# Choosing experts for two token blocks at a time in an attention and mixture-of-experts kernel

## The chip, the core and the metric

The kernel runs on one core of a Trainium2 chip. The metric is the device time of one launch in microseconds (us). A core has five engines that run side by side, each through its own instruction stream in order: TensorE (PE, matrix products), VectorE (DVE), ScalarE (ACT), GpSimd (POOL), and SyncE (SP), which here issues DMAs. Engines wait for one another by semaphores.

## What is computed

The reference is one transformer layer in fp32 on 4096 tokens of width 256: attention over the whole causal sequence, and then a mixture of 8 experts of which each token takes 2.

```python
x = x + attention(layernorm(x), Qw, Kw, Vw)          # one head, causal
h = layernorm(x) @ W_in + b_in
probs = softmax(h @ W_gate + b_gate)                 # 8 experts
topv, topi = top_k(probs, 2)
topv = topv / topv.sum(-1, keepdims=True)            # the two shares
mid = relu(einsum('nd,edh->neh', h, W1) + b1)        # expert width 1024
eout = einsum('neh,ehd->ned', mid, W2) + b2
moe = sum over the two chosen experts of share * eout
out = x + moe @ W_out + b_out
```

## The kernel before

**Tiles and stages.** The 4096 tokens are 8 blocks of 512 (`NB`), each of 4 tiles of 128 tokens (`TPB`). Queries go in 16 groups of 256, two to a block; group `g` belongs to block `b = g // 2`, and `q = g % 2`. The main loop (L1036) runs over the groups. In each round it issues the scores of the next group (`scores`, L500, products `ps` at L516), a transposition of the running maxima and the subtraction of the maximum (`finish`, L554: `pt`, the reduction `m` at L563, `pmax`, the subtractions L572 and L578, Exp on ACT), and then the weighted sums of the present group (`attend`, L585, products `po` at L593, with rescaling at L605 and L607).

**What goes with the first group of a block** (`q == 0`). `enter(b - 1)` (L314) takes the normalized rows of the block before, forms `h` and the 8 logits of each token in one product (`ph`, L323) and adds the biases on DVE: the logits to `lg` (L333), the rows to `hr`, which SP writes to DRAM. Behind `attend` come the projection and the values of the next block (`pq` L472, `pv` L487), and then `route(b - 1)` (L347), then the statistics of block `b + 2`.

**`route`** chooses the experts of one block. Its DVE instructions work on all four tiles at once, as 128 partitions by 4 tokens by 8 experts, thus 32 columns:
- L360 to L375: the largest logit, its subtraction, an Exp on ACT (L362), twice the largest probability with a one-hot row of the expert that has it (`hot`; ties go by `rank`), and `both`, the sum of the two. Fourteen of these instructions follow one from another.
- L377 to L381: `past`, the running count of tokens per expert and partition; it begins with `seen` of the block before, and each further tile needs the one before it. The last one is the next `seen`.
- L384 and L389: two products on PE into `pk`, which turn `both` and `past` into each token's place in the list of its expert.
- L393 to L402: the place is added to the expert's first slot (`first`), picked out by `hot`, summed, and cast to integers `ati`.
- L404: eight scatters per block by POOL, which write the number of the assignment to its slot in DRAM.
- L416 to L419: the shares of the two experts.

The small tiles of `route` have two buffers. Block 6 is routed inside the last block's sums (`find`, L1072) and block 7 in the expert stage (L1209).

**Order.** The sequence of the text is what the compiler's scheduler starts from; it moves instructions within an engine by dependencies and by its own estimate of when each is ready. Some are held in program order by hand (`keep_in_program_order`). An engine then executes its order strictly.

**After the loop's start for block 7.** `early = seen` (L1051) takes the counts of blocks 0 to 5; `plan("a", ...)` (L1052) builds from them a table of work pieces of 256 slots. The expert stage (L1177) then runs over the pieces: fetch slots, gather rows, two products with the expert's weights (`pm`, `pe`), scatter. Last come the output products (`pa`, `pf`).

Of the kernel before, what the change touches and what calls it, by code (L numbers as in the profile page):

```python
# [10 lines left out]
F32 = mybir.dt.float32  # L11
I32 = mybir.dt.int32
AF = mybir.ActivationFunctionType
ALU = mybir.AluOpType
# [3 lines left out]
P = 128  # L18
# [6 lines left out]
SH = 128  # L25
SQR = 64
TOPK = 2
LINE = 16
SQ = 32
LATE = 2  # L30
# [7 lines left out]
def preln_attention_moe_kernel(  # L38
# [18 lines left out]
    nc = tc.nc  # L57

    _, S, D = x.shape
    NE, _, FF = W1.shape  # L60
    NT = S // P
    NB = S // TB
    TPB = TB // P
# [24 lines left out]
    const = ctx.enter_context(tc.tile_pool(name="const", bufs=1))  # L88
    stream = ctx.enter_context(tc.tile_pool(name="stream", bufs=1))
    dram = ctx.enter_context(tc.tile_pool(name="dram", bufs=1, space=bass.MemoryType.DRAM))  # L90
    attn = ctx.enter_context(tc.tile_pool(name="attn", bufs=1))
# [218 lines left out]
    share = [const.tile([P, NT], F32, tag=f"share{k}", name=f"share{k}") for k in range(TOPK)]  # L310
    seen = const.tile([P, NE], F32, tag="seen0", name="seen0")
    nc.gpsimd.memset(seen, 0.0)

    def enter(b, zT, pool, behind=False):  # L314


        hr = pool.tile([P, TPB, D], F32, tag="hr", name=f"hr{b}", bufs=1)

        lg = pool.tile([P, TPB, NE], F32, tag="lg", name=f"lg{b}", bufs=2)
        for j in range(TPB):  # L320
            ph = ps_mm(f"ph{b}_{j}")
            for c in range(ND):
                done = nc.tensor.matmul(  # L323
                    ph[:, :DG],
                    lhsT=zT[:, c, ts(j, P)],
                    rhs=win_sb[:, c, :],
                    start=(c == 0),
                    stop=(c == ND - 1),
                )
                if behind:  # L330
                    tc.keep_in_program_order(done)
                    behind = False
            nc.vector.tensor_tensor(lg[:, j, :], ph[:, D:DG], bgate_bc, ALU.add)  # L333
            nc.vector.tensor_tensor(hr[:, j, :], ph[:, :D], bin_bc, ALU.add)
        for k in range(TOPK):
            put = nc.sync.dma_start(
                out=rows[ts(b, TOPK * TB), :].rearrange("(t p k) d -> p t k d", p=P, k=TOPK)[
                    :, :, k, :
                ],
                in_=hr,  # L340
            )
            if b == NB - 1:
                tc.add_to_no_dep_group("last", put.ins)

        return lg

    def route(b, lg, seen, pool, behind=False):  # L347


        def small(name, w=1):  # L350
            return pool.tile([P, TPB, w], F32, tag=name, name=f"{name}{b}", bufs=2)

        def wide(a):
            return a.to_broadcast([P, TPB, NE])


        top = [small(f"top{k}") for k in range(TOPK)]
        hot = [small(f"hot{k}", NE) for k in range(TOPK)]
        prob, best = small("prob", NE), small("best")
        nc.vector.tensor_reduce(best, lg, AX.X, ALU.max)  # L360
        nc.vector.tensor_tensor(lg, lg, wide(best), ALU.subtract)
        nc.scalar.activation(prob, lg, AF.Exp)  # L362
        left = prob
        for k in range(TOPK):
            nc.vector.tensor_reduce(top[k], left, AX.X, ALU.max)
            nc.vector.tensor_tensor(hot[k], left, wide(top[k]), ALU.is_equal)
            nc.vector.tensor_tensor(hot[k], hot[k], rank, ALU.mult)
            nc.vector.tensor_reduce(best, hot[k], AX.X, ALU.max)
            nc.vector.tensor_tensor(hot[k], hot[k], wide(best), ALU.is_equal)
            if k == 0:  # L370
                left = small("left", NE)
                nc.vector.scalar_tensor_tensor(left, hot[0], -2.0, prob, ALU.mult, ALU.add)

        both = small("both", NE)
        nc.vector.tensor_tensor(both, hot[0], hot[1], ALU.add)  # L375
        past = small("past", NE)
        nc.vector.tensor_copy(past[:, 0, :], seen)  # L377
        for j in range(1, TPB):
            nc.vector.tensor_tensor(past[:, j, :], past[:, j - 1, :], both[:, j - 1, :], ALU.add)
        now = const.tile([P, NE], F32, tag=f"seen{b + 1}", name=f"seen{b + 1}")  # L380
        nc.vector.tensor_tensor(now, past[:, TPB - 1, :], both[:, TPB - 1, :], ALU.add)  # L381
        pk = ps_tr(f"pk{b}") if behind else ps_o(f"pk{b}")
        pkv = pk[:, : TPB * NE]
        done = nc.tensor.matmul(  # L384
            pkv, lhsT=before, rhs=both.rearrange("p t e -> p (t e)"), start=True, stop=False
        )
        if behind:
            tc.keep_in_program_order(done)
        nc.tensor.matmul(  # L389
            pkv, lhsT=ones, rhs=past.rearrange("p t e -> p (t e)"), start=False, stop=True  # L390
        )
        place = small("place", NE)
        nc.vector.tensor_tensor(  # L393
            place, pkv.rearrange("p (t e) -> p t e", e=NE), first, ALU.add
        )
        for k in range(TOPK):
            nc.vector.tensor_tensor(hot[k], hot[k], place, ALU.mult)
            at, ati = small(f"at{k}"), pool.tile(
                [P, TPB], I32, tag=f"ati{k}", name=f"ati{k}_{b}", bufs=2
            )  # L400
            nc.vector.tensor_reduce(at, hot[k], AX.X, ALU.add)
            nc.vector.tensor_copy(ati, at[:, :, 0])  # L402
            for j in range(TPB):
                put = nc.gpsimd.indirect_dma_start(  # L404
                    out=slots,
                    out_offset=bass.IndirectOffsetOnAxis(ap=ati[:, j : j + 1], axis=0),
                    in_=assign[:, TOPK * (b * TPB + j) + k :][:, :LINE],
                    in_offset=None,
                )

                tc.declare_no_dep(put.ins, group="slots", reason="slots are distinct")
                tc.add_to_no_dep_group("slots", put.ins)
                if b == NB - 1:
                    tc.add_to_no_dep_group("last", put.ins)
        tot = small("tot")
        nc.vector.tensor_tensor(tot, top[0], top[1], ALU.add)  # L416
        nc.vector.reciprocal(tot, tot)
        for k in range(TOPK):
            nc.vector.tensor_tensor(  # L419
                share[k][:, ts(b, TPB)], top[k][:, :, 0], tot[:, :, 0], ALU.mult  # L420
            )
        return now

# [564 lines left out]
    before = const.tile([P, P], F32, tag="before", name="before")  # L988
    make_upper_triangular(nc, before, 1.0, diag=False)

    rank = const.tile([P, TPB, NE], F32, tag="rank", name="rank")

    first = const.tile([P, TPB, NE], F32, tag="first", name="first")
    number = const.tile([P, NE], F32, tag="number", name="number")
    for e in range(NE):
        nc.gpsimd.memset(rank[:, :, e : e + 1], float(NE - e))
# [38 lines left out]
    fill, lg, got, hTs = [], None, {}, {}  # L1035
    for g in range(NT // KU):  # L1036
# [12 lines left out]
        if q == 0 and b == NB - 1:  # L1049
# [3 lines left out]
            for n in range(AHEAD + 1):  # L1053
                got[n] = fetch_rows(work[n])
        if q == 0 and b > 0:

            def send(behind=False):
                nonlocal lg
                lg = enter(b - 1, z1T, attn, behind)

            if b - 1 < TURNED[1]:
                turn(1, b - 1, rows1, z1T)
                send()
            else:
                between[5] = [partial(send, True)]
        if q == 0 and b == NB - 1:

            def fetch_first():
                for n in range(AHEAD):
                    got[n] += fetch_weights(work[n])  # L1070

            def find():  # L1072
                nonlocal seen
                seen = route(b - 1, lg, seen, attn, True)

            between[6], between[11] = [fetch_first], [find]
            weighed = AHEAD
        elif q == 0 and b + 1 < TURNED[0]:
            turn(0, b + 1, ahead, zT[b + 1])
        attend(g, row, between)  # L1080
        row = nxt
        if q == 0 and b + 1 < NB:
            project(b + 1)
            values(b + 1)
            if b > 0:
                seen = route(b - 1, lg, seen, attn)
        if q == 0 and b + 2 < NB:
            stats0(b + 2)
            by_dve = b + 2 >= TURNED[0]
# [87 lines left out]
    for n, item in enumerate(work):  # L1177
# [26 lines left out]
            following, behind = hidden(work[n + 1], got[n + 1], hTs.pop(n + 1), behind)  # L1204
        if n == 0:
            turn(1, NB - 1, rows1, z1T)
            lg = enter(NB - 1, z1T, attn)
        if n == 1:
            seen = route(NB - 1, lg, seen, attn)  # L1209
            tables["z"], seen = plan_late(seen, early)  # L1210
            tables["b"] = plan("b", seen, NBLK - NFULL, SB, SQR - 1, tables["a"][2])

            def twice(k):
                taken = const.tile([P, NE], F32, tag="twice" + k, name="twice" + k)
                nc.vector.tensor_scalar_mul(taken, tables[k][2], 2.0)
                return taken

            tables["c"] = plan("c", seen, NHALF, SH, SQR - 1, twice("b"))
            tables["d"] = plan("d", seen, 2 * NPAIR, SQR, SQR - 1, twice("c"))
# [59 lines left out]
```

## Time and profile before

| what | value |
|---|---|
| median of 3 runs | 1087.06 us (1086.69 to 1088.53) |
| profiled execution | 1081.01 us |
| its span, first to last instruction | 1079.2 us |
| mean granted TensorE clock | 1.000 |
| PE waits for `ph`, one at 53 us | 1.2 us |
| count products L384 and L389 | 16 and 16 records of 128x32, 2.6 and 3.0 us |
| scatters L404 | 64, 62.9 us on POOL, 983 ns each |
| one DVE instruction of 128x32 in `route` | 0.18 to 0.19 us |

The span is what lies between the first and the last instruction of one profiled execution; its own time has 1.8 us around it. A product in fp32 is two records in the trace. The duration of a matmul record covers its pipeline, so records overlap, and the distance from start to start is what a record costs the stream. Where an engine was idle before an instruction, the timeline gives the idle time and the event that ended it in brackets.

### The profile page before, as it was taken

To read this page: it belongs to the slowest core of one execution; us is meant where nothing else is said; L and a number is where in the kernel's file an instruction comes from. 1 tells how busy PE (TensorE), PEld (TensorE's weight loads), DVE (VectorE), ACT (ScalarE), POOL (GpSimd) and SP (SyncE) were. 2 spreads that over 40 slices of the span, in tenths; PEclk is the share of its full clock that TensorE was granted. 3 is DMA by queue.
4 is the path that set the end of the run, shared out by engine and by line. 5 is a ranking of instruction groups with operands and counts; after the bars stand their busy time and mean duration, and the time that the engine had idled before them with its cause. 6 is when DMAs were issued, how large, how long until landed. Compare 5 with 4: busy or idle time off the path is not lost. (4 is left out here: it accounts for less than half of the span.)

```text
span 1079.2 us, 15699 instructions
## 1 busy us (share of the span) xinstructions
PE 1069.7 (99%) x5013; PEld 889.7 (82%) x5013; DVE 728.9 (68%) x2260; ACT 332.2 (31%) x731; POOL 238.4 (22%) x293
## 2 busy tenths in 40 slices
PE   9999999999999999999999999999999999999998
PEld 6878888888888888888888887787878777777887
DVE  5777788778676658255774743858588876767636
ACT  2222333332332323242402222232322432323254
POOL 2122312103103010201132522232222332313110
PEclk9999999999999999999999999999999999999999
DMA  9111001001001001000645474888879796979285
GB/s 329 59 42 40 3 1 42 1 11 32 1 1 42 1 1 40 3 1 0 187 144 181 155 241 148 274 276 259 290 253 330 254 337 208 332 224 327 80 294 189
DMA packets 121416, 151.96 MB, mean 141 GB/s; under 512 B 25581, under 2 KB 101298, under 8 KB 121332
## 3 DMA queue, kind: packets, MB, share of 16 engines
q1 hardware_dynamic: 112404, 132.84, 37.6%
q0 software_dynamic: 8384, 17.58, 5.1%
q8 instruction: 40, 0.66, 0.2%
q10 hardware_dynamic: 544, 0.52, 0.1%
q14 instruction: 44, 0.36, 0.1%
HBM read 124.79 MB, written 26.38 MB: 140 GB/s over the span
## 5 line engine op out<-in xcount | busy, mean ns | idle before, releaser
L593 PE MATMUL po<-v,s 128*128 128x257 f32 x1056 | 237.8, 380 | 0.0
L516 PE MATMUL ps<-qT,zT 128*128 128x256 f32 x1088 | 233.6, 374 | 0.0
L516 PEld LDWEIGHTS ps<-qT,zT 128*128 128x128 f32 x1088 | 203.4, 191 | 27.6 <-issue 1.3
L593 PEld LDWEIGHTS po<-v,s 128*128 128x128 f32 x1056 | 197.4, 190 | 26.2
L525 ACT COPY s<-ps 128x512 f32<-128x512 f32 x120 | 70.2, 585 | 170.7 <-PE ps L516 131.2
L948 PE MATMUL pe_a<-w_a,mid_a 128*128 128x256 f32 x544 | 121.6, 381 | 0.0
L881 PE MATMUL pm_a<-hT_a,w_a 128*128 128x256 f32 x544 | 120.0, 380 | 0.0
L948 PEld LDWEIGHTS pe_a<-w_a,mid_a 128*128 128x128 f32 x544 | 102.9, 190 | 18.7 <-issue 5.6
L890 ACT ACTIVATE mid_a<-pm_a,c_a 128x256 f32<-128x256 f32 x136 | 64.2, 472 | 169.3 <-PE pm_a L881 147.6
L881 PEld LDWEIGHTS pm_a<-hT_a,w_a 128*128 128x128 f32 x544 | 103.6, 190 | 13.8
L575 ACT ACTIVATE s<-s 128x512 f32<-128x512 f32 x120 | 71.7, 629 | 83.4 <-DVE s L572 83.1
L531 DVE TENSOR_TENSOR mx<-ps,mx 128x512 f32<-128x512 f32 x91 | 62.9, 691 | 50.8 <-ACT s L525 48.0
L861 DVE STREAM_TRANSPOSE hT_a<-h_a 32x128 f32<-32x128 f32 x272 | 82.2, 302 | 4.0
L404 POOL DMA_INDIRECT slots<-assign,ati x64 | 62.9, 983 | 84.2 <-DVE ati L402 65.6
L572 DVE TENSOR_TENSOR s<-s,pmax 128x512 f32<-128x512 f32 x120 | 73.1, 682 | 7.3 <-PE pmax L568 7.3
L957 POOL DMA_INDIRECT parts<-y_a,slot_a x34 | 34.2, 1006 | 168.2 <-DVE y_a L956 139.0
L853 DVE STREAM_TRANSPOSE mid_c<-raw_c 32x256 f32<-32x256 f32 x128 | 55.8, 436 | 1.9
L948 PE MATMUL pe_b<-w_b,mid_b 128*128 128x256 f32 x256 | 56.8, 380 | 0.0
L881 PE MATMUL pm_b<-hT_b,w_b 128*128 128x256 f32 x256 | 56.6, 380 | 0.0
L948 PEld LDWEIGHTS pe_b<-w_b,mid_b 128*128 128x128 f32 x256 | 48.6, 190 | 9.3 <-issue 2.6
L881 PEld LDWEIGHTS pm_b<-hT_b,w_b 128*128 128x128 f32 x256 | 48.7, 190 | 6.5
L890 ACT ACTIVATE mid_b<-pm_b,c_b 128x256 f32<-128x256 f32 x64 | 30.1, 471 | 63.0 <-PE pm_b L881 63.0
(283 smaller groups left out, 1232.9 us busy)
## 6 DMA issues: line engine op xcount, KB each, us to landing
w_a<-in_L_ffn_W_dram SPq DMA_DIRECT2D x68, 512.0 KB, 5.0
w_d<-in_L_ffn_W_dram SPq DMA_DIRECT2D x48, 512.0 KB, 5.4
w_c<-in_L_ffn_W_dram SPq DMA_DIRECT2D x32, 512.0 KB, 6.9
w_b<-in_L_ffn_W_dram SPq DMA_DIRECT2D x32, 512.0 KB, 7.4
rows<-hr SPq DMA_DIRECT2D x16, 512.0 KB, 4.1
yp<-parts SPq DMA_DIRECT2D x14, 512.0 KB, 11.2
x<-in_L_attn_x_dram SPq DMA_DIRECT2D x7, 512.0 KB, 7.0
out_dram<-ot SPq DMA_DIRECT2D x14, 256.0 KB, 5.2
```

The source lines that it names most:

```text
L404: put = nc.gpsimd.indirect_dma_start(out=slots, out_offset=bass.IndirectOffsetOnAxis(ap=ati[:, j : j + 1], axis=0), in_=assign[:, TOPK * ( ...
L516: nc.tensor.matmul(ps[:, u * QB + lo : (u + 1) * QB], lhsT=zT[kt // TPB][:, d, ts(kt % TPB, P)], rhs=qT[b][:, d, q * QB + lo : (q + 1) * Q ...
L525: nc.scalar.copy(flat, ps)
L531: done = nc.vector.tensor_tensor(mx, ps, old, ALU.max)
L572: nc.vector.tensor_tensor(s, s, pm[:, :QB].unsqueeze(1).to_broadcast([P, KU, QB]), ALU.subtract)
L575: nc.scalar.activation(s, s, AF.Exp)
L593: nc.tensor.matmul(po[u][:, : D + 1], lhsT=ss[c][:, k, ts(u, P)], rhs=vb[kt // TPB][:, kt % TPB, :], start=(kt == 0), stop=(kt == g * KU + u),
L853: pin(do())
L861: pin(do())
L881: nc.tensor.matmul(pm[:, :SB], lhsT=w1[c][:, ts(f, P)], rhs=hT[:, c, :], start=(c == 0), stop=(c == ND - 1),)
L890: nc.scalar.activation(mid[f // 2][:, f % 2, :], pm[:, :SB], AF.Relu, bias=c1[:, f : f + 1])
L948: nc.tensor.matmul(pe[ts(j, rest), :D], lhsT=mid[f][:, ts(u, P)][:, ts(j, rest)], rhs=w2[f // (NF // 2)][:, f % (NF // 2), :], start=(f == 0),
```

## The change

Blocks 0 and 1, 2 and 3, and 4 and 5 are routed together, at the place where blocks 1, 3 and 5 were routed. Blocks 6 and 7 are routed alone as before. A new constant `ROUTED = 2` gives the number of blocks in a set.
- The logits of two blocks lie in one tile `lg` of 8 tokens by 8 experts per partition, and `enter` is given its half.
- `route(b, n, ...)` takes `n` blocks: its instructions have 64 columns where `n` is 2, the chain of `past` has 7 additions where it had 3 for each block, `pk` is one pair of products of 64 columns, and 16 scatters follow one another.
- The small tiles have room for two blocks and one buffer where they had two.
- `rank` and `first`, which POOL fills at the start, are twice as wide.

```diff
+ROUTED = 2
...
-    def enter(b, zT, pool, behind=False):
+    def enter(b, zT, pool, lg, behind=False):
...
-        lg = pool.tile([P, TPB, NE], F32, tag="lg", name=f"lg{b}", bufs=2)
...
+    def logits(b):
+        return attn.tile([P, ROUTED * TPB, NE], F32, tag="lg", name=f"lg{b}", bufs=2)
+
+    def route(b, n, lg, seen, pool, behind=False):
+
+        nt = n * TPB
 
         def small(name, w=1):
-            return pool.tile([P, TPB, w], F32, tag=name, name=f"{name}{b}", bufs=2)
+            t = pool.tile([P, ROUTED * TPB, w], F32, tag=name, name=f"{name}{b}", bufs=1)
+            return t[:, :nt, :]
...
-        for j in range(1, TPB):
+        for j in range(1, nt):
             nc.vector.tensor_tensor(past[:, j, :], past[:, j - 1, :], both[:, j - 1, :], ALU.add)
-        now = const.tile([P, NE], F32, tag=f"seen{b + 1}", name=f"seen{b + 1}")
-        nc.vector.tensor_tensor(now, past[:, TPB - 1, :], both[:, TPB - 1, :], ALU.add)
+        now = const.tile([P, NE], F32, tag=f"seen{b + n}", name=f"seen{b + n}")
+        nc.vector.tensor_tensor(now, past[:, nt - 1, :], both[:, nt - 1, :], ALU.add)
         pk = ps_tr(f"pk{b}") if behind else ps_o(f"pk{b}")
-        pkv = pk[:, : TPB * NE]
+        pkv = pk[:, : nt * NE]
...
-            nc.vector.tensor_copy(ati, at[:, :, 0])
-            for j in range(TPB):
+            nc.vector.tensor_copy(ati[:, :nt], at[:, :, 0])
+            for j in range(nt):
                 put = nc.gpsimd.indirect_dma_start(
...
-                share[k][:, ts(b, TPB)], top[k][:, :, 0], tot[:, :, 0], ALU.mult
+                share[k][:, b * TPB :][:, :nt], top[k][:, :, 0], tot[:, :, 0], ALU.mult
...
-    rank = const.tile([P, TPB, NE], F32, tag="rank", name="rank")
-
-    first = const.tile([P, TPB, NE], F32, tag="first", name="first")
+    rank = const.tile([P, ROUTED * TPB, NE], F32, tag="rank", name="rank")
+
+    first = const.tile([P, ROUTED * TPB, NE], F32, tag="first", name="first")
...
+            if (b - 1) % ROUTED == 0:
+                lg = logits(b - 1)
 
             def send(behind=False):
-                nonlocal lg
-                lg = enter(b - 1, z1T, attn, behind)
+                enter(b - 1, z1T, attn, lg[:, (b - 1) % ROUTED * TPB :][:, :TPB, :], behind)
...
-                seen = route(b - 1, lg, seen, attn, True)
+                seen = route(b - 1, 1, lg[:, :TPB, :], seen, attn, True)
...
-            if b > 0:
-                seen = route(b - 1, lg, seen, attn)
+            if b > 0 and b % ROUTED == 0:
+                seen = route(b - ROUTED, ROUTED, lg, seen, attn)
...
-            lg = enter(NB - 1, z1T, attn)
+            lg = logits(NB - 1)
+            enter(NB - 1, z1T, attn, lg[:, :TPB, :])
...
-            seen = route(NB - 1, lg, seen, attn)
+            seen = route(NB - 1, 1, lg[:, :TPB, :], seen, attn)
```

More of the change, by code (lines that the diff above doesn't have):

```diff
@@ L343, in enter @@
                 tc.add_to_no_dep_group("last", put.ins)
-        return lg
-    def route(b, lg, seen, pool, behind=False):
+    def logits(b):
+        return attn.tile([P, ROUTED * TPB, NE], F32, tag="lg", name=f"lg{b}", bufs=2)
+    def route(b, n, lg, seen, pool, behind=False):
+        nt = n * TPB
         def small(name, w=1):
-            return pool.tile([P, TPB, w], F32, tag=name, name=f"{name}{b}", bufs=2)
+            t = pool.tile([P, ROUTED * TPB, w], F32, tag=name, name=f"{name}{b}", bufs=1)
+            return t[:, :nt, :]
         def wide(a):
-            return a.to_broadcast([P, TPB, NE])
+            return a.to_broadcast([P, nt, NE])
         top = [small(f"top{k}") for k in range(TOPK)]
@@ L366, in route @@
             nc.vector.tensor_tensor(hot[k], left, wide(top[k]), ALU.is_equal)
-            nc.vector.tensor_tensor(hot[k], hot[k], rank, ALU.mult)
+            nc.vector.tensor_tensor(hot[k], hot[k], rank[:, :nt, :], ALU.mult)
             nc.vector.tensor_reduce(best, hot[k], AX.X, ALU.max)
@@ L393, in route @@
         nc.vector.tensor_tensor(
-            place, pkv.rearrange("p (t e) -> p t e", e=NE), first, ALU.add
+            place, pkv.rearrange("p (t e) -> p t e", e=NE), first[:, :nt, :], ALU.add
         )
@@ L398, in route @@
             at, ati = small(f"at{k}"), pool.tile(
-                [P, TPB], I32, tag=f"ati{k}", name=f"ati{k}_{b}", bufs=2
+                [P, ROUTED * TPB], I32, tag=f"ati{k}", name=f"ati{k}_{b}", bufs=1
             )
             nc.vector.tensor_reduce(at, hot[k], AX.X, ALU.add)
-            nc.vector.tensor_copy(ati, at[:, :, 0])
-            for j in range(TPB):
+            nc.vector.tensor_copy(ati[:, :nt], at[:, :, 0])
+            for j in range(nt):
                 put = nc.gpsimd.indirect_dma_start(
@@ L412, in route @@
                 tc.add_to_no_dep_group("slots", put.ins)
-                if b == NB - 1:
+                if b + n == NB:
                     tc.add_to_no_dep_group("last", put.ins)
```

## The prediction

> **What bounds the kernel now.** I read the page first, then the groups by shape, then TensorE's waits, then the timelines of TensorE (PE), VectorE (DVE) and GpSimd (POOL) around each set of choices.
>
> ```profile
> PE 1069.7 (99%) x5013; PEld 889.7 (82%) x5013; DVE 728.9 (68%) x2260; ACT 332.2 (31%) x731; POOL 238.4 (22%) x293
> ```
>
> PE is the bound over the whole span, and its order is fixed. What the change takes out of PE's stream, or makes PE wait for, is time; DVE's 32% of idle time hides what happens on DVE unless PE waits for it. The list of PE's waits is short, and two of its entries belong to the count products:
>
> ```profile
> PE pk L384 <- DVE both L375: 1.1, 1, 1.1
> PE pk L389 <- DVE past L379: 0.3, 1, 0.3
> ```
>
> Asked by windows, the first lies at 545 to 552 us (block 6, chosen alone before and after), the second at 60 to 80 us (block 0). In the timelines the columns are start, length, engine, line. Lengths of matmuls overlap (a 128x256 record is 0.38 long, yet one starts every 0.216 us), so I price by starts. Four places on PE:
>
> ```profile
> 70.75 0.30 PE L384 MATMUL pk<-both,before 128*128 128x32 f32 x2
> 71.32 0.41 PE L389 MATMUL pk<-past,ones 128*128 128x32 f32 x2 [0.27 <-DVE past L379]
> 71.56 2.62 PE L516 MATMUL ps<-qT,zT 128*128 128x256 f32 x11
> ...
> 118.11 0.30 PE L384 MATMUL pk<-both,before 128*128 128x32 f32 x2
> 118.25 0.39 PE L389 MATMUL pk<-past,ones 128*128 128x32 f32 x2
> 118.47 1.76 PE L516 MATMUL ps<-qT,zT 128*128 128x256 f32 x7
> ...
> 176.65 1.46 PE L516 MATMUL ps<-qT,zT 128*128 128x256 f32 x6
> 178.23 0.38 PE L384 MATMUL pk<-both,before 128*128 128x32 f32 x2
> 178.44 0.68 PE L516 MATMUL ps<-qT,zT 128*128 128x256 f32 x2
> 178.96 0.30 PE L389 MATMUL pk<-past,ones 128*128 128x32 f32 x2
> ```
>
> At 118 us nothing is waited for: from the first pk to the first ps is 0.36 us, and that ps takes 0.083 us over its usual 0.216 because its weights were not loaded ahead. At 70 us there is a wait inside. At 177 us the sixth ps starts at 177.73 (five steps of 0.216), so pk could start at 177.95 and starts at 178.23: 0.28 of wait.
>
> The DVE chain that feeds them, where it stands before work that PE wants (block 1), and where it has little slack (block 3):
>
> ```profile
> 107.20 0.19 DVE L375 TENSOR_TENSOR both<-hot,hot 128x32 f32<-128x32 f32 x1
> 107.43 0.57 DVE L379 TENSOR_TENSOR past<-past,both 128x8 f32<-128x8 f32 x3
> 108.03 0.17 DVE L381 TENSOR_TENSOR seen<-past,both 128x8 f32<-128x8 f32 x1
> 108.23 0.17 DVE L377 COPY past<-seen 128x8 f32<-128x8 f32 x1
> 108.31 0.42 DVE L563 TENSOR_REDUCE m<-pt 128x2 f32<-128x256 f32 x1
> ...
> 248.33 0.19 DVE L375 TENSOR_TENSOR both<-hot,hot 128x32 f32<-128x32 f32 x1
> 248.56 0.57 DVE L379 TENSOR_TENSOR past<-past,both 128x8 f32<-128x8 f32 x3
> ```
>
> Dependent small instructions start 0.20 to 0.22 us apart, independent ones about 0.09. At block 1, PE stands still some 0.30 us before its pmax transposes at 108.78 (four po from 107.61 are issued by 108.48), since m comes late behind the chain.
>
> [...] here four records of 128x32 take 0.446 us with the late ps, 0.111 each, so the loads set the price and not the 32 columns. [...] a pk that waits holds everything behind it, as at 70 us. [...] The trace has 182 to 188 for 128x32 rows and 211 to 220 for its 128x64 rows (L649, L655 of the plans): I take 0.03 us more for a doubled width.
>
> **The change part by part.** DVE and PE orders of both kernels agree except for the chains and the pk; SP's order is the same.
>
> *Removed on PE*: the products at blocks 0, 2 and 4, by the starts of single records in the trace. Block 0: from the first pk at 70.746 to the second ps record at 71.860 is 1.114, less one step of 0.216: 0.90 (0.43 of it wait). Block 2: from the ps record at 177.730 to the fourth ps record behind it at 179.399 (both pk lie between) is 1.67, less four steps, 0.86: 0.81 (0.28 of it wait). Block 4 is like 118 us: 0.45. Sum 2.15 us.
>
> *Kept but wider*: three pairs of 64 columns. 64 columns stream in less than the 0.109 us at which 128-column transposes start, which is below the weight load's 0.111. I take 0; the upper end is 27 ns more for each of six products, 0.16.
>
> *Pair of blocks 0 and 1* (at 104 us). Fourteen instructions from L360 to L375 get 64 wide: 14 x 0.03 = 0.42 later. But the new DVE order puts m behind the second past, where the old had three past, seen and the copy ahead: past 2 starts at 107.63, so m could follow at 107.72, 0.59 earlier. Net 0.17 earlier, and the 0.30 of PE wait shrinks by that. The other five past stand in front of the L572 subtractions: about 1 us, of which 0.53 was idle anyway (DVE waits for pmax there), so DVE runs some 0.3 behind PE's pace; the output rescaling L607 that frees PSUM for the pv products has about 0.45 of room (first one done 114.2, pv at 114.66). I take 0; lower cover would cost up to 0.15.
>
> *Pair 2, 3* (at 242 us). The chain is mixed with statistics and copies; both comes 0.42 later (end 248.94) and PE asks for it at 249.40: no wait. past is seven long instead of three, 4 x 0.20 = 0.80 more: it ended at 249.13 and ends at 250.35. The new PE order places one ps product between the two pk, so L389 is wanted 0.73 after L384, as at 178 us: 250.13. Wait 0.22. The split costs two switches instead of one, 0.08 (0.81 - 0.28 - 0.45). Together 0.30. Queued behind the waiting pk are only ps products; DVE's place L393 and what follows come about 1 us later, while the first PSUM tile that PE needs back from DVE (by L531) is four ps tiles, some 7 us, further on.
>
> *Pair 4, 5* (at 423 us). past would have ended near 428 against pk at 435.7: no wait.
>
> *DVE*: three chains less, about 28 instructions each; on no path but the waits named. *ACT*: three Exp less, three wider: none of them on PE's path. *POOL*: 64 scatters as before, but 16 in a row instead of 8. They start 1.265 us apart, so 20.2 us from 119.8 to 140.1. Behind them in the queue:
>
> ```profile
> 144.84 0.23 POOL L249 TENSOR_SCALAR ln1rstd<-ln1mv 128x4 f32<-128x4 f32 x1 [15.10 <-DVE ln1mv L243]
> ```
>
> It has 4.7 us of room; after the other pairs 16 and 30. *Startup memsets* of double width: POOL is idle for 7.35 us before 19.09. *Single buffers* in place of two: the last readers, the scatters, are done at least 30 us before the next writer (562 against 594 us for the two blocks chosen alone; over 80 us for the pairs). The last pair's scatters land near 458; the tables that read the slots are made from 508 on: nothing.
>
> *Sum*: -2.15 - 0.17 + 0.30 = -2.0 us. Against the profiled execution: 1081.01 (span 1079.2 and 1.8 around it) to 1079.0. The median of the runs shown is 6 us above that execution; I carry the difference over unscaled: 1087.06 - 2.0 = 1085.0.
>
> **The rivals.**
>
> A, as above, 1085.0, its own range 1084.4 to 1085.8 from the unknown ends (+0.16, +0.15, the wait at 250 us between 0 and 0.6): chance 0.58. It lies beside the bound of 0.2% (2.17 us), which is about what a measurement of this kernel can tell from no change; I give 0.30 beyond it and 0.28 within.
>
> B, more: with DVE freed, a larger wait that DVE causes shrinks as well, the 1.29 us at 545.7 before block 6's pk. For it: a DVE chain is what is late there. Against: that stretch has the same order and the same instructions, and DVE is driven by PE's own scores. 1083.7; chance 0.22, since the freed DVE touches many short waits that I can't list.
>
> C, less: the two removed waits (0.43 and 0.28) were cover for something, and PE stops at its next consumer instead. Then only three bare pairs of products go: -3 x 0.45 - 0.17 + 0.30 = -1.2, 1085.9. Against: at both places DVE loses work before that consumer. 0.10.
>
> D, slower: the doubled width costs DVE more than 0.03, at the two places where PE hangs on the chain. With w per instruction the sum is -2.15 + (14w - 0.59) + (14w + 0.80 - 1.00) + 0.08; it turns at w = 0.10. At double price, w = 0.185, it is +2.3: 1089.4. Against it are the 128x64 rows at 0.21 to 0.22. 0.10.
>
> That the change doesn't do what it says is ruled out by the order: six pk instructions fewer, 81 fewer on DVE.
>
> **How the numbers follow.** Faster 0.30 + 0.22 = 0.52; same 0.28 + 0.10 = 0.38; slower 0.10. The range, 1083.4 to 1086.9, holds A, B and C with the half us by which medians differ, and leaves out D and about as much at the tails.
>
> **What would show it.** Right: the wait at 70 us and the stop at 177.7 are gone, no pk stands at blocks 0, 2, 4; the pair of 64 columns without a wait takes 0.36 us to the first ps; a wait of 0.2 to 0.3 us for past near 248 us; 128x64 chain rows at 0.21 to 0.22. Wrong: chain rows above 0.3 us, a wait of over 1 us at the second pair or at pmax near 106 us, ln1rstd waiting for scatters, or a changed wait at block 6.

## The result, and the profile after

| | kernel before | changed kernel | ratio (95% interval) |
|---|---|---|---|
| comparison of the result, 6 runs each | 1088.61 us (1086.69 to 1092.04) | 1108.22 us (1106.2 to 1110.23) | 1.0181 (1.0166 to 1.0195) |
| profiled execution | 1081.01 us, span 1079.2 | 1106.74 us, span 1105.0 | |

The changed kernel is 1.8% slower, where 2 us less were forecast. One thing in the table bears on all that follows: the profile of the kernel before is of an execution of 1081 us, while its timed runs need 1087 to 1092 us. The experiments show that both belong to the same program under two conditions, which I call undisturbed (before at 1081.1) and disturbed (before at 1088.6). Each comparison below lay wholly within one of them, on one chip: undisturbed on the chips numbered 2, 14, 13 and 9, disturbed on those numbered 2 and 5.

The busy times of the page after, PE to POOL:

```profile
span 1105.0 us, 15591 instructions
PE 1077.1 (97%) x5001; PEld 889.7 (81%) x5001; DVE 720.5 (65%) x2182; ACT 331.3 (30%) x728; POOL 238.0 (22%) x293
```

The instructions went nearly as foreseen: 12 records fewer on PE, 3 fewer on ACT, and 78 fewer on DVE where 81 were forecast. Yet PE stands idle for 28 us where it had 9.5. The places that the prediction priced, in PE's timeline of the changed kernel (start, length, engine, line, operation, count):

```profile
69.19 1.46 PE L489 MATMUL pv<-vw,zT 128*128 128x256 f32 x6
70.49 2.32 PE L518 MATMUL ps<-qT,zT 128*128 128x256 f32 x10
...
116.85 0.33 PE L386 MATMUL pk<-both,before 128*128 128x64 f32 x2
117.02 0.39 PE L391 MATMUL pk<-past,ones 128*128 128x64 f32 x2
117.24 1.08 PE L518 MATMUL ps<-qT,zT 128*128 128x256 f32 x4
...
254.03 0.33 PE L386 MATMUL pk<-both,before 128*128 128x64 f32 x2
254.19 0.65 PE L518 MATMUL ps<-qT,zT 128*128 128x256 f32 x2
254.85 0.43 PE L391 MATMUL pk<-past,ones 128*128 128x64 f32 x2
```

The wait and the two products at 70 us are gone; from the first product of 64 columns to the first ps are 0.39 us. But the last stretch, for which PE asked at 249.40 in the kernel before, begins at 254.03, 4.6 us late instead of 2 early. The list of PE's waits in the changed kernel (us in total, times, longest) has entries that the kernel before doesn't have:

```profile
PE ps L518 <- DVE mx L533: 8.2, 3, 5.1
PE po L595 <- issue: 4.2, 6, 1.5
PE pm_a L883 <- ACT mid_a L892: 2.7, 1, 2.7
PE pt L560 <- issue: 2.2, 2, 1.1
```

"issue" means that nothing which the profile shows was waited for. How such a stop comes about is seen on ACT, which copies scores from PSUM behind PE. ACT's timeline of the changed kernel in the second row of 16 scatters, with the idle time before each copy and what ended it:

```profile
261.85 0.59 ACT L527 COPY s<-ps 128x512 f32<-128x512 f32 x1 [1.14 <-PE ps L518]
263.58 0.59 ACT L527 COPY s<-ps 128x512 f32<-128x512 f32 x1 [1.14 <-issue]
266.90 0.59 ACT L527 COPY s<-ps 128x512 f32<-128x512 f32 x1 [2.73 <-remote]
272.59 0.59 ACT L527 COPY s<-ps 128x512 f32<-128x512 f32 x1 [5.10 <-PE ps L518]
279.66 1.56 ACT L527 COPY s<-ps 128x512 f32<-128x512 f32 x3 [6.49 <-remote]
```

and PE's own timeline there:

```profile
264.24 7.93 PE L518 MATMUL ps<-qT,zT 128*128 128x256 f32 x36
273.95 1.57 PE L518 MATMUL ps<-qT,zT 128*128 128x256 f32 x8 [1.77 <-DVE mx L533]
275.36 0.60 PE L595 MATMUL po<-v,s 128*128 128x257 f32 x2
277.50 0.38 PE L595 MATMUL po<-v,s 128*128 128x257 f32 x1 [1.54 <-issue]
```

PE made scores up to 272 us, yet ACT's copies of them come 5.7 and 7.1 us apart where they came every 1.73 us. PE then runs out of free PSUM tiles (DVE's `mx` is late as well), and at last two of its own products start 1.9 us apart with nothing open. By 281 us ACT has caught up. POOL's timeline shows what else ended just before:

```profile
274.72 0.96 POOL L406 DMA_INDIRECT slots<-assign,ati  x1 [0.30 <-issue]
275.98 0.96 POOL L406 DMA_INDIRECT slots<-assign,ati  x1 [0.30 <-issue]
```

The sixteenth scatter starts at 275.98. Late copies and stops of PE stand at the other two rows of 16 as well. The scatters themselves keep their pace, 1.265 us from one to the next.

### The profile page after: what moved, and what is told of

Same layout as the page of the kernel before. It is cut to its first block, busy times and chain, and to the rows that moved or that the text cites. A ratio compares the mean times of both kernels' runs of the same rounds, so it can differ in the third digit from the quotient of the medians.

```text
span 1105.0 us, 15591 instructions
## 1 busy us (share of the span) xinstructions
PE 1077.1 (97%) x5001; PEld 889.7 (81%) x5001; DVE 720.5 (65%) x2182; ACT 331.3 (30%) x728; POOL 238.0 (22%) x293
## 5 line engine op out<-in xcount | busy, mean ns | idle before, releaser
L595 PE MATMUL po<-v,s 128*128 128x257 f32 x1056 | 242.0, 383 | 4.2 <-issue 4.2
```

The source lines that it names most:

```text
L595: nc.tensor.matmul(po[u][:, : D + 1], lhsT=ss[c][:, k, ts(u, P)], rhs=vb[kt // TPB][:, kt % TPB, :], start=(kt == 0), stop=(kt == g * KU + u),
```

## The experiments

Theories: BURST (a row of more than some eight scatters delays what other engines do), CHAIN (the 64-wide chain with its single buffers and later `past`), and others as they came up. Where two kernels are compared by PE's starts, the record starts of PE in the two traces are matched one by one, and the growth of their distance over a stretch is given.

### A pause between the scatters, first attempt

```diff
+                if n == ROUTED and k * nt + j in PAUSES:
+                    for _ in range(PAUSE):
+                        nc.gpsimd.tensor_tensor(idle, idle, half[:, :TPB], ALU.pow)
                 put = nc.gpsimd.indirect_dma_start(
```

`PAUSES` is (8,), (4, 8, 12) and (12,); `PAUSE` is 6, 2 and 6.

> The changed kernel, with a pause of six tiny powers on GpSimd (six by 1.04 us = 6.2 us by the row of ln0rstd) between scatter 8 and scatter 9 of each pair; nothing else. BURST (more than some 8 scatters without a pause delay the signals between the engines, and each scatter beyond costs time): the pause brings the three losses at 135-144, 271-281 and 462-475 us down to near nothing, 1086 to 1090 us. CHAIN (the 64-wide chain, its single buffers or its two products cost the time): all of that is unchanged, 1107 to 1109 us. HELD QUEUE (GpSimd occupied for longer delays what comes behind it): worse than the changed kernel, as the scatters end 6.2 us later, above 1109.

> The changed kernel with the same 6.2 us of pause for each pair, but as three pauses of two powers (2.1 us) after scatters 4, 8 and 12. If it is the mean rate of scatters over some 20 us that counts, as in the run with one pause, 1086 to 1090 us. If a backlog builds up from the first scatter on and needs several us of rest to drain, short pauses help less than the one long pause: between that run and 1108 us. CHAIN: 1107 to 1109 us.

> The changed kernel with the one pause of 6.2 us after scatter 12. BURST with a threshold near 8: scatters 9 to 12 still cost, a third to a half of the loss stays, 1093 to 1099 us. If it begins at 13 (the first stall in the changed kernel is seen 17 us after the first scatter, which is the 13th or 14th), the loss is gone: 1086 to 1090 us. CHAIN: 1107 to 1109 us.

Measured: 1093.35, 1093.91 and 1093.33 us beside 1081.05 (ratios 1.0108 [1.0091, 1.0125], 1.0117 [1.0100, 1.0134], 1.0108 [1.0091, 1.0124]). None tested its theory. The powers depend on nothing in the chain, and the scheduler put all 18 at the start. POOL's timeline of the first of them:

```profile
14.27 18.36 POOL L410 TENSOR_TENSOR idle<-idle,half 128x4 f32<-128x4 f32 x17
32.62 0.24 POOL L252 TENSOR_SCALAR ln0rstd<-ln0mv 128x4 f32<-128x4 f32 x1
```

The second block's norms, ln0rstd, stand behind them in POOL's queue and PE waits 12.6 us for these. The useful part is the rest: the scatters of all three still stood 16 in a row, and by PE's starts none of them lost anything there.

### Scatters 16 in a row in the kernel before, first attempt

```diff
-            for j in range(TPB):
+            held.append((b, k, ati))
+        for c, k, ati in held if b % 2 or b == NB - 2 else ():
+            for j in range(TPB):
```

> The kernel before with its own 32-wide chain for each block, but the 8 scatters of blocks 0, 2 and 4 are kept back and issued ahead of those of blocks 1, 3 and 5, so that they stand 16 in a row at the places where the changed kernel has them. BURST: the losses of the changed kernel appear with nothing of its chain in the kernel, 1106 to 1111 us. CHAIN: as the kernel before, 1087 to 1090 us.

Measured: 1081.13 us beside 1081.05, ratio 1.0002 (0.9995 to 1.0009). The scheduler undid it: the held scatters were ready, and POOL issued them by eights at the old places. It says nothing on either theory. From here on an order is forced by data, not by the place in the text.

### The changed kernel again; a true row of 16 in the kernel before; a true pause

For the row of 16, the indexes of the even block are made from those of the odd one, times nothing:

```diff
+                for c, l, old, oldi in held:
+                    nc.vector.scalar_tensor_tensor(
+                        oldi, at[:, :, 0], 0.0, old[:, :, 0], ALU.mult, ALU.add
+                    )
```

For the pause, six powers start from the first block's indexes, and the second block's indexes are made from their end:

```diff
+                nc.gpsimd.tensor_scalar(idle, ati[:, :TPB], 0.0, 1.0, ALU.mult, ALU.add)
+                for _ in range(PAUSE):
+                    nc.gpsimd.tensor_tensor(idle, idle, half[:, :TPB], ALU.pow)
+                for l, (i, f) in enumerate(held):
+                    nc.vector.scalar_tensor_tensor(
+                        i[:, TPB:nt], idle, 0.0, f[:, TPB:nt, 0], ALU.mult, ALU.add
+                    )
```

> The changed kernel as it is, once more, beside the kernel before. In the runs with a pause the powers went to the start of the kernel, where they held POOL for 18 us and put off the second block's norms by 12.6 us; the scatters stayed 16 in a row, and yet the three losses at the scatters weren't there. If the loss belongs to the kernel, it comes again: 1.8% above the kernel before, the signals of PE to ACT late in the three stretches. If it belongs to the chip or to the execution that was measured first, this run shows the local gains alone: 1.4 us under the kernel before.

> The kernel before with its own chains of 32 columns, but the indexes of blocks 0, 2 and 4 are made from those of blocks 1, 3 and 5 (plus nothing times them), so that their 8 scatters can't be issued before, and 16 stand in a row where the changed kernel has them. Adds two DVE operations of 128x4 for a pair. BURST: the losses of the changed kernel appear here, 20 us or more above the kernel before. CHAIN, or a cause outside of both: as the kernel before within 0.5 us.

> The changed kernel with a true pause: the second block's 8 indexes of a pair are made from the end of six powers on POOL (6.2 us) that start from the first block's, so that the scatters stand as 8, a pause of some 8 us, and 8. BURST: no loss, 1.5 us under the kernel before whatever the changed kernel shows on this chip. CHAIN: as the changed kernel on this chip, with or without the loss.

Measured, beside 1081.1 us: the changed kernel 1078.9 (0.9983, interval 0.9975 to 0.9991); the row of 16 in the kernel before 1081.14 (0.9998, 0.9989 to 1.0007); the pause 1112.06 (1.0289, 1.0272 to 1.0306). The same changed kernel now gains 2.2 us. In ACT's timeline the copies keep their step through the whole row:

```profile
258.61 0.59 ACT L527 COPY s<-ps 128x512 f32<-128x512 f32 x1 [1.14 <-PE ps L518]
260.34 0.59 ACT L527 COPY s<-ps 128x512 f32<-128x512 f32 x1 [1.14 <-PE ps L518]
262.07 0.59 ACT L527 COPY s<-ps 128x512 f32<-128x512 f32 x1 [1.14 <-PE ps L518]
```

CHAIN falls here: the chain, its buffers and its products are all in this kernel, and nothing is lost. BURST as a property of the program falls too. The pause kernel was slow for a reason of its own. DVE's timeline:

```profile
135.65 0.23 DVE L431 SCALAR_TENSOR_TENSOR ati<-idle,at 128x4 int32<-128x4 f32 x2 [12.15 <-POOL idle L429]
```

DVE stood 12.15 us at the instruction that waits for the end of the powers, and PE's scores, which DVE takes from PSUM, behind it (25.2 us of PE waits for `mx` over the three pairs). By PE's starts against the changed kernel run beside it, the three places lost 11.9, 10.6 and 10.8 us, which is all of the 33 us between the two: each stop, and after it products at a granted clock of 0.50. It is a mistake of the experiment, and a good picture of what one waiting instruction does to a strict queue.

### The same on a disturbed chip

The next comparison met the other condition: the kernel before stood at 1088.62 us. The pause is now made on POOL alone, which no other engine waits for; the double kernel issues each scatter of pairs 2/3 and 4/5 twice:

```diff
+                nc.gpsimd.tensor_scalar_add(idle, idle, -1.0)
...
-                    nc.vector.scalar_tensor_tensor(
-                        i[:, TPB:nt], idle, 0.0, f[:, TPB:nt, 0], ALU.mult, ALU.add
-                    )
+                    nc.gpsimd.tensor_tensor(f[:, TPB:nt, 0], idle, f[:, TPB:nt, 0], ALU.add)
+                    nc.gpsimd.tensor_copy(i[:, TPB:nt], f[:, TPB:nt, 0])
...
-            for j in range(nt):
+            for j in 2 * list(range(nt)) if n == ROUTED and b > 0 else range(nt):
```

> The changed kernel a third time. The first comparison had it 20 us above the kernel before, with signals late at the scatters; the second had it 2.1 us below, with none late, on another chip. CHIP (the late signals belong to the chip or to its condition in that hour): where the kernel before stands at 1081 us, 1078.9 us again; where it stands at 1087 to 1092 us, some 1106 to 1110 us. KERNEL (it has two ways to run, by chance): single executions of both kinds on one chip.

> The kernel before with its chains as they are, and the scatters of two blocks 16 in a row, again. On a chip where the kernel before stands at 1081 us: 1081. On one where it stands at 1087 to 1092 us: BURST says that it loses as the changed kernel does, above 1106 us; CHAIN that it stays with the kernel before.

> The changed kernel with 8 scatters, a pause of some 7 us on POOL, and 8 scatters for a pair. This time POOL itself makes the second block's indexes at the end of the pause, so that no DVE instruction waits for it: in the run before, 1112 us, PE stopped at such a wait three times (8.9, 8.1 and 8.8 us). If that is where those 33 us came from: as the changed kernel within 0.5 us on a chip with the kernel before at 1081. On a disturbed chip BURST says 2 us under the kernel before; CHAIN 20 us above it.

> The changed kernel with every scatter of pairs 2/3 and 4/5 issued twice (the second writes the same numbers to the same slots): 32 in a row, 40.5 us. BURST on any chip, if only the row is long enough: losses of 10 us and more at 267-291 and 452-476 us, and signals late at ACT. Otherwise only ln1rstd of pair 2/3, due at 286 us, waits behind the scatters until some 290.7: 4 to 5 us at most, and nothing at pair 4/5, where ln1rstd is due 10 us after the last scatter.

Measured: the changed kernel 1107.79 us (1.0180, 1.0163 to 1.0197); the kernel before with its scatters 16 in a row 1109.62 (1.0197, 1.0180 to 1.0214); the pause 1087.75 (0.9994, 0.9985 to 1.0003); the double rows 1148.07 (1.0550, 1.0526 to 1.0573). The pause can't be told from the kernel before, where BURST had said 2 us less: by PE's starts against the version with a rest of 2 us, which follows below, its rows lose 1.1, 0 and 0 us, the 1.1 because ln1rstd stands behind the last scatter. POOL works all through that pause (six powers of 1.1 us, one behind another), so what costs is not that POOL is busy but that it scatters. ACT's timeline of the kernel before with 16 in a row, which has none of the changed chain:

```profile
266.55 0.59 ACT L539 COPY s<-ps 128x512 f32<-128x512 f32 x1 [1.14 <-issue]
269.21 0.58 ACT L539 COPY s<-ps 128x512 f32<-128x512 f32 x1 [2.07 <-PE ps L530]
276.34 0.58 ACT L539 COPY s<-ps 128x512 f32<-128x512 f32 x1 [6.54 <-PE ps L530]
282.02 1.56 ACT L539 COPY s<-ps 128x512 f32<-128x512 f32 x3 [5.10 <-remote]
```

These are delays as in the changed kernel: the last copies start 2.7, 7.1 and 5.7 us apart, where they were 3.3, 5.7 and 7.1. In the disturbed condition BURST holds, and CHAIN has nothing left. With 32 in a row, ACT makes a single copy between 270.92 and 300.47 us (the last scatter starts at 295.96):

```profile
282.92 0.59 ACT L527 COPY s<-ps 128x512 f32<-128x512 f32 x1 [11.41 <-remote]
300.47 0.59 ACT L527 COPY s<-ps 128x512 f32<-128x512 f32 x1 [16.97 <-remote]
```

### How long a rest, where, and whose queue

Three kernels: the changed one with only the six small POOL operations between the eights, some 2 us; 12 scatters, the pause of 7 us, and 4; and the kernel before with 24 small transfers from SyncE's queue beside the 8 scatters of blocks 1, 3 and 5:

```diff
+            for i in range(24):
+                put = nc.sync.dma_start(
+                    out=scratch[ts(i, P), :TPB], in_=spare[:, :TPB]
+                )
```

> The changed kernel with 8 scatters, only the six small POOL operations that make the second block's indexes, some 2 us between the end of one scatter and the start of the next, and 8 scatters. The pause of 7 us (1087.75 us where the kernel before had 1088.62) ended the losses at the scatters, but put ln1rstd of pair 0/1 off by 1.5 us, to 148.6. DRAIN (what backs up behind a row of scatters is gone within 2 us): where the kernel before stands at 1087 to 1092 us, no loss at the scatters and 1086.0 to 1087.0 us, below both kernels; SLOW DRAIN: the second eight still cost, 1092 to 1106 us. Where the kernel before stands at 1081 us: as the changed kernel, 1079 us.

> The changed kernel with 12 scatters, the pause of 7 us, and 4. On a disturbed chip (before at 1087 to 1092 us): if only what comes after the twelfth or thirteenth scatter of a row costs, as the first stalls of the changed kernel say (17 us after the first scatter), 1087 to 1089 us; if every scatter beyond eight costs its share, 3 to 4 us for each pair more, 1096 to 1101 us. On an undisturbed one 1079 to 1080 us.

> The kernel before, with 24 small transfers (128 pieces of 16 bytes) from SyncE's queue to a spare buffer after the chains of blocks 1, 3 and 5, beside their 8 scatters; no scatter is moved. On a disturbed chip: if it is the number of small transfers and of their 16 signals each, whoever issues them, losses as in the changed kernel or greater, 1105 us and more; if it takes POOL's own queue, as the kernel before within 2 us, 1087 to 1092 us. On an undisturbed one: 1081 us either way.

Undisturbed again: 1078.93 us beside 1081.14 (0.9981, 0.9972 to 0.9989), 1080.03 (0.9990, 0.9983 to 0.9996) and 1081.11 (1.0000, 0.9991 to 1.0008). The 7 us of pause delay ln1rstd of the first pair and so cost about a microsecond against the 2 us; the rest is as it was without a pause. The first and the third were run again:

> The changed kernel with 8 scatters, 2 us of small POOL operations, and 8, again: the last run met an undisturbed chip, 1078.9 us. On a disturbed one (before at 1087 to 1092 us): DRAIN, 1086.0 to 1087.0 us and no loss at the scatters; SLOW DRAIN, 1092 to 1106 us with PE stopping from the third or fourth scatter of the second eight on. On an undisturbed one 1078.9 us again.

> The kernel before with 24 small transfers from SyncE's queue beside the 8 scatters of blocks 1, 3 and 5, again. On a disturbed chip: by the number of small transfers and their signals, 1105 us and more; by POOL's own queue, 1087 to 1092 us, as the kernel before. On an undisturbed one 1081 us.

1078.89 beside 1081.12 (0.9981, 0.9974 to 0.9987) and 1081.11 (1.0001, 0.9993 to 1.0010), undisturbed once more. And a third time:

> The version with 8 scatters, 2 us of small POOL operations, and 8 a third time, as the two before met undisturbed chips (1078.9 us in both). On a disturbed chip (before at 1087 to 1092 us): DRAIN, 1086.0 to 1087.0 us; SLOW DRAIN, 1092 to 1106 us. Otherwise 1078.9 us.

> The kernel before with 24 small transfers from SyncE's queue a third time, for the same reason. On a disturbed chip: by the number of small transfers and their signals 1105 us and more; by POOL's own queue 1087 to 1092 us. Otherwise 1081 us.

This time the kernel before stood at 1088.55. The eights with 2 us between took 1084.57 us (0.9973, 0.9965 to 0.9981), below both kernels, and less than the 1086.0 that was expected. The SyncE transfers took 1090.49 (1.0015, 1.0001 to 1.0030), far from 1105, yet above the kernel before. POOL's and ACT's timelines of the eights with a rest:

```profile
258.87 0.96 POOL L360 DMA_INDIRECT slots<-assign,ati  x1 [0.30 <-issue]
259.90 0.19 POOL L426 TENSOR_SCALAR idle<-ati 128x4 f32<-128x4 int32 x1
260.18 0.23 POOL L427 TENSOR_SCALAR idle<-idle 128x4 f32<-128x4 f32 x1
260.49 0.35 POOL L429 TENSOR_TENSOR at<-idle,at 128x4 f32<-128x4 f32 x2
260.78 0.32 POOL L430 CAST ati<-at 128x4 int32<-128x4 f32 x2
261.64 1.08 POOL L360 DMA_INDIRECT slots<-assign,ati  x1 [0.54 <-issue]
```

```profile
256.71 0.59 ACT L544 COPY s<-ps 128x512 f32<-128x512 f32 x1 [1.14 <-issue]
259.83 0.59 ACT L544 COPY s<-ps 128x512 f32<-128x512 f32 x1 [2.53 <-PE ps L535]
261.32 1.16 ACT L544 COPY s<-ps 128x512 f32<-128x512 f32 x2 [0.90 <-PE ps L535]
263.62 0.59 ACT L544 COPY s<-ps 128x512 f32<-128x512 f32 x1 [1.14 <-PE ps L535]
```

One copy is 1.4 us late at the end of the first eight (3.12 after the one before it, not 1.73); in the rest all is caught up, and PE loses nothing.

## Why the prediction was wrong

What each row cost, by PE's starts in a disturbed trace against the same kernel undisturbed (for the SyncE kernel, against the kernel before), in us:

| kernel in the disturbed condition | first row, 119 us | second, 250 us | third, 436 us | block 6, 545 to 575 us | 612 to 650 us |
|---|---|---|---|---|---|
| changed, 16 in each row | 6.7 | 5.2 | 8.8 | 2.5 | 4.7 |
| before, 16 in each row | 7.9 | 4.8 | 9.3 | 0.9 | 4.7 |
| changed, 16, 32, 32 | 6.4 | 26.6 | 27.7 | 2.6 | 4.7 |
| changed, 8, rest of 2 us, 8 | 0 | 0 | 0 | 0.9 | 4.7 |
| before, and 24 from SyncE | 1.8 | 0 | 0 | 2.5 | 4.9 |

The rows of 16 cost 20.7 us and that is the result: 1108.22 - 1088.61 = 19.6 is what they cost less the gain of about 2 us, to within 1 us. The last column is the same in all kernels, and block 6 lies between 0.9 and 2.6: there POOL has gathers and scatters closely one behind another in the kernel before too, though no run tests that they are the cause. In the last row of the table the two columns make 7.3 us. The kernel before itself is 7.5 us slower in this condition (1088.55 against 1081.05); no disturbed trace of it is on record. Doubling a row adds 19 to 21 us for 16 more scatters, 1.2 to 1.3 each, about the 1.265 us from one scatter to the next: while the longer row goes on, PE stands nearly all of the time.

Point by point, by the prediction's steps:

- **Removed products.** Right, to the hundredth: from the kernel before to the changed kernel undisturbed, block 0 gave 0.90, block 2 0.81 and block 4 0.45 us, which were the three numbers. The disturbed profile has the same.
- **Wider products at nothing.** Right: from the first pk to the ps behind the second 0.39 us, with 32 columns 0.36. The two traces, at 118 us before and at 117 us after, show what sets the price: from the second record of the first pk to the first ps the weight loads start 0.110 to 0.112 us apart in both widths, and the products 0.111 to 0.112. Only the first pk's second record follows its first sooner, after 0.028 us with 32 columns and 0.056 with 64, which is the difference. The late ps at 118 us starts 0.028 us after its load, the ps record behind it 0.216.
- **Pair 0/1, 0.17 earlier.** Right in kind; 0.11.
- **Pair 2/3, +0.30.** Right; 0.27. Pair 4/5 free: right.
- **Sum.** 2.0 us were forecast against the profiled execution of 1081.01, so 1079.0. The changed kernel undisturbed took 1078.9. Of the 2.1 us between the two traces 2.0 arise at the places named.
- **Rival D, DVE's double width.** Its price is refuted: 128x64 rows of the chain last 0.22 us, against 0.19 for 128x32 (a median of 191 ns, where the prediction read 182 to 188).
- **POOL: "64 scatters as before, but 16 in a row instead of 8".** This is the step that failed. It was priced by POOL's own queue: the end of the row against ln1rstd, with 4.7 us of room, so nothing. That is true of POOL (ln1rstd waited for DVE and not for scatters) and beside the point. In the disturbed condition the row costs the other engines: from the end of its eighth scatter on ACT's copies come late (in each of the three rows the first late copy starts 10.1 us after the first scatter, as 266.90 after 256.83), PE stops some us later, and the term was 20.7 us instead of 0.
- **"I carry the difference over unscaled."** Here the sign was passed over. The 6 us between the median (1087.06) and the profiled execution (1081.01) were treated as a constant around the kernel. By the last row of the table they were stops in block 6 and the expert stage, absent from the trace that was read. They are a sign of the condition in which longer rows on POOL bring new stops, and no constant could carry these.

None of the rivals had this mechanism.

**What is shown, and what isn't.** Shown: the loss depends on a condition of the machine that holds through a whole comparison, and not on the change alone (the chip numbered 2 had the kernel before at 1081.05 in one comparison and at 1088.62 in another, 27 minutes later); in that condition the length of a row of scatters decides, with either chain; a rest of 2 us after eight removes it. 24 transfers from SyncE within 12.5 us cost PE 1.8 us at one place of three, so it isn't the mere number of small transfers. They aren't without effect: beside them ACT's late copies start 5.6, 4.1 and 3.6 us after the one before, where rows of eight alone have 2.7, 3.1 and 2.7. These transfers have 128 packets of 16 bytes where a scatter has 16 of 512, so whether it takes POOL's queue, the form of its transfers or their pace isn't settled. The row of 12 and 4 was not met in the disturbed condition, so the length from which PE loses time is only known to lie between 8 and 16; ACT's first late copy comes at the end of the eighth, also in rows that cost PE nothing.

Not settled: what the condition is, and what stops the engines. One trace of it can be had: how many of a scatter's increments of its semaphore were recorded. In the trace of the kernel before, 188 of the 196 transfers that POOL issues have 16, and 390 of SyncE's 398. Counted in two traces of the changed kernel (the run beside the true pause, and the one beside the double rows), second row:

```
undisturbed  16 16 16 16 16 16 16 16 16 16 16 16 16 16 16 16
disturbed    16  6  3  4  7  4  2  3  4  7  2  3  1  3  3  2
```

All semaphore records together are 12,983 against 9,928 (in the profiles of the first comparison 13,074 before and 9,950 after). The waits on these semaphores were satisfied (in the profile after, the scatters of the third row wait on them and start from 447.52 us on, 1.265 us apart), so the increments took place and only their records are missing, also in rows of eight that cost nothing. The other records agree: both traces have 15,591 instructions and 121,429 DMA packets, and the 256 data packets of this row, 512 bytes each, take 62 ns on average in both, so the scatters' own transfers are no slower. Whether the taking of records has a part in the stops is not shown: the timed executions were recorded as well (the record has a span and a clock for each), so that whether an unrecorded one would stop isn't known.

## What to carry to other kernels

When the timed runs lie several microseconds above the profiled execution, with a spread that can't explain it, the profile may show another condition than the times do, as here: ask what differs before carrying the distance over as a constant, and compare at more than one time. A row of scatters on POOL is not free because POOL is (each row of 16 cost 4.8 to 9.3 us in the disturbed condition): keep rows short, or put other small POOL work after every eight, which here cost nothing undisturbed (0.9981) and made the change a gain in both conditions (0.9973 disturbed). That holds for recorded executions, the only ones measured. And an order that only the text gives is not an order: the four kernels whose pauses or rows weren't tied by data were put in another order by the scheduler.

## What the runs showed of the hardware

- In the disturbed condition engines stopped with nothing open: ACT was idle for 17 us before a copy, until 4.5 us after the start of the last of 32 scatters. In that row PE's own products start 1.4, 2.1, 2.8 and 3.5 us apart, nearly all of them close to multiples of 0.7 us; in the first row of the changed kernel, from 137.27 us on, 1.41, 1.41, 0.71 and 0.70.
- After some of these stops PE runs at half pace. PE's timeline of the eights with a rest, at 613 us:

```profile
613.13 3.62 PE L900 MATMUL pm_a<-hT_a,w_a 128*128 128x256 f32 x16
619.50 5.37 PE L900 MATMUL pm_a<-hT_a,w_a 128*128 128x256 f32 x16 [2.75 <-ACT mid_a L909]
```

  The same 16 products take 1.75 us more after 2.75 us of idle time: about eight of them start at twice the usual 0.216 us. The changed kernel's trace has the same at 642 us: after 2.71 us of idle time seven of the products start 0.43 us apart, and the granted clock is 0.50 from 642.77 us on, for 3.4 us. Nor does it take a single long stop: in the first row of the changed kernel PE is busy for 0.83 us between 137.60 and 141.01 and never idle for more than 1.2 us at a time, and its granted clock is 0.50 for the 3.4 us after. In the second row, which cost 5.2 us, the clock stays at 1.00. The changed kernel's stretches at 0.50 last 17.1 us together (the mean granted clock is 0.992, undisturbed 1.000), so by estimate at most half of that, 8.5 us, is paid after the stops and not in them.
- A DVE instruction of 0.2 us that waited 12.15 us for POOL stopped PE for 8.7 us (8.68 of idle time before the next ps).
